# A rational-form attention on Trainium2: late key tiles ordered by a table of times, one exponential for two reciprocals, four banks in turn for the numerators

## The chip, the cores and the metric

The kernel runs on one core of one Trainium2 chip. The metric is the device time of one execution in microseconds (us); the profile's span is the time from the first to the last instruction of one profiled execution. Engine names are those of the profile: PE (matrix multiply), PEld (its weight loads), DVE (vector), ACT (activations), POOL (GpSimd), SP (the queue that issues most DMAs).

## The reference, cut to what matters

A network of two layers on x of shape (4, 128, 64, 64): a convolutional state-space layer, then an additive attention and a recurrent layer over 4096 tokens of 128 channels. The change touches the attention alone.

```python
def _L1_attn_ref(x, Wt, Wx, bh, Wa, ba):            # x: (4, 4096, 128), layer-normed tokens
    q = jnp.einsum('bld,ud->blu', x, Wt)            # 32 units u
    k = jnp.einsum('bld,ud->blu', x, Wx)
    beta = jnp.tanh(q[:, :, None, :] + k[:, None, :, :] + bh)
    alpha = jnp.einsum('bsju,u->bsj', beta, Wa[:, 0]) + ba[0]
    alpha = jnp.tanh(alpha)
    alpha = jax.nn.softmax(alpha, axis=-1)
    return jnp.einsum('bsj,bjd->bsd', alpha, x)

t = t + _L1_attn_ref(_ln_t(t), Wt, Wx, bh, Wa, ba)
t = t + _L1_ffn_ref(_ln_t(t), W, V, gamma, beta)
```

## The kernel before, in words

`_bounded` runs three stages one after the other, each with an order of instructions written out by hand: `_layer0` (the convolutional layer), `_rational` (the attention) and `_chunked` (the recurrent layer). The change is inside `_rational`.

The sum of tanh over 32 units is computed as a sum of fractions. The units are cut into groups of 6, 6, 5, 5, 5 and 5. For a group, exponentials of all signed sums of its units (64 or 32 rows) are kept for the keys (`F`) and for the queries (`E`). The product of `F` and `E` over the rows of a group is the fraction's denominator (`lower`, into a two-bank PSUM tile `pd`), and the product of `F` with the weighted `cE` is its numerator (`upper`, into two one-bank tiles `pn`). Unit A holds the two groups of 64 rows, B1 and B2 two groups of 32 rows each; B1 lies in rows 0 to 63 of PE's array, B2 in rows 64 to 127.

The work is tiled by batch `b` (4), by 512 queries (`s`, 8 per batch, so 32 query tiles) and by 128 keys (`jt`, 32 per query tile). For one `jt`:

- PE computes dA, dB1, dB2 (denominators) and nA, nB1, nB2 (numerators) (line 1212);
- ACT inverts each denominator by a logarithm (line 1231) and an exponential of its negative (line 1232), 1024 elements each, into `ra` (A) or `rb` (B1, B2);
- DVE multiplies with the numerators, two instructions of 512 elements per unit (`times`, line 1227; below xA, xB1, xB2);
- POOL adds B1 to A (line 1346; the first add), then B2 (line 1333; the second add);
- DVE adds the two halves into `A[:, jt, :]` (line 1343; below f).

The work of B2 and f belongs to the next pass of the loop over `jt`. So the order of one pass is: PE dA, nB2 of the pass before, dB1, nA, dB2, nB1; DVE xB2 of the pass before, xA, xB1, f of the pass before. The queues run in order; buffers set who waits. `psD` has two `pd` tiles, `psN` three `pn` banks, `psW` one bank (`ct`) for everything else; `ra` has three tiles, `rb` four.

At the end of a query tile ACT applies tanh and exp to `A` in four parts (lines 1381, 1382; another table is loaded before and the first one after, line 1068). Meanwhile `ahead` does the first `jt` of the next query tile with DVE reciprocals (`direct`, lines 1239, 1240), for which it needs the next `cE` (`weigh`, line 1200). The weighted sum over the keys (`weighted`, line 1357) is a chain of 32 matmuls into `ct`: the first 20 run at the end of the tile, the last 12 one by one in jt 2 to 13 of the next tile.

Other small pieces are hung into the loop by the dictionary `between`, behind the work of a given `jt`: the closing of the last query tile (copy of `ct`, a matmul for the softmax's denominators, four reciprocals, a matmul for the numerators, a POOL add and the output's DMA; `CLOSE_AT`), the layer norm of the next batch's tokens (`NORM_AT`: centre, square, rate, scale; not in the last batch) and the next tile's `E` (`QUERIES_AT`).

## Time and profile before

| What | Value |
|---|---|
| Time, median of 3 runs | 11655.28 us (11652.04 to 11657.58) |
| Profiled execution: its time | 11654.41 us |
| Profiled execution: span | 11652.7 us, mean granted PE clock 0.939 |
| Attention stage | about 4044 to 11430 us of the span, 32 query tiles |
| L1231, logarithm of 1024 (`rb`) | x1986, mean 1011 ns |
| L1232, exponential of 1024 (`rb`) | x1986, mean 1057 ns |
| L1382, exponential of 2048 (tile end) | x31, mean 1910 ns |
| L1227, DVE multiply of 512 (`rb`) | x3972, mean 682 ns |
| L1346 / L1333, POOL's first / second add of 1024 | x993 each, mean 2653 / 2363 ns |
| L1343, DVE's sum f | x993, mean 750 ns |
| L1239, DVE reciprocal of 512 | x186, mean 3351 ns |

The first stage (to about 4044 us) and the last one (from about 11430 us) hold none of the lines that the change touches. A line of the profile's timeline gives start, duration, engine, line, operation, output and input, count, and in brackets the idle time before it with what ended it; "L1212" is line 1212 of the kernel. Matmul durations overlap, so on PE the distance between starts is what counts.

### The profile page before, as it was taken

The page shows a single profiled execution, that of the slowest core. Times are in us where ns is not written, and L with a number is a line of the kernel's source. Part 1 is how long each engine was busy: PE and PEld are TensorE (multiplying, and loading weights), DVE is VectorE, ACT ScalarE, POOL GpSimd, SP SyncE. Part 2 cuts the span into 40 slices and gives each one's busy share as a digit, 9 for nine tenths or more (in the row PEclk, how much of TensorE's full clock was granted, in tenths as well). Part 3 has the DMA queues.
Part 4 walks back from the last instruction along what each step waited for, and adds up shares of the span by engine and source line. Part 5 has one row for each costly group of instructions (what it writes and reads, how often), then busy time and mean ns, then how long its engine had stood idle before and what let it go on. Part 6 is the DMA issues. An engine that isn't in the chain of part 4 may idle for free.

```text
span 11652.7 us, 111820 instructions
## 1 busy us (share of the span) xinstructions
PE 10307.6 (88%) x36210; PEld 3184.3 (27%) x36210; DVE 8997.6 (77%) x10066; ACT 9520.9 (82%) x10209; POOL 8625.1 (74%) x3703
## 2 busy tenths in 40 slices
PE   6787787778777699999999999999999999999997
PEld 2121121122111133333333333333333333333334
DVE  4998899889889677777777777777777777777773
ACT  3566556656655599999999999999999999999996
POOL 3999889889889677767766776767677767776773
PEclk8898898889888799999999999999999999999998
DMA  4888778778778300000000000000000000000001
GB/s 118 189 182 194 171 177 193 170 182 190 179 171 186 79 1 3 6 3 3 6 3 3 3 6 3 3 3 6 3 3 3 6 2 3 3 4 3 2 3 60
DMA packets 225332, 737.77 MB, mean 63 GB/s; under 512 B 41104, under 2 KB 41936, under 8 KB 223712
## 3 DMA queue, kind: packets, MB, share of 16 engines
q1 hardware_dynamic: 221760, 729.96, 26.5%
q8 instruction: 286, 4.69, 0.2%
q14 instruction: 310, 2.54, 0.1%
q10 hardware_dynamic: 2976, 0.58, 0.0%
HBM read 612.95 MB, written 117.44 MB: 63 GB/s over the span
## 4 chain that ended last, share of the span: by engine, by line
PE 50%; ACT 9%; DVE 4%; issue 3%; POOL 0%; DMA 0%; DVEq 0%; POOLq 0%; SPq 0%; ACTq 0%
PE pn L1212 26%; PE pd L1212 16%; PE ct L1357 4%; ACT A L1381 3%; ACT A L1382 2%; DVE rb L1227 2%; ACT rb L1231 1%; ACT rb L1232 1%; PE ct L1134 1%; ACT ra L1231 1%; DVE rb L1239 1%; PE vy L1556 0%; DVE A L1343 0%; PE pn L56 0%; PE ct L1262 0%
## 5 line engine op out<-in xcount | busy, mean ns | idle before, releaser
L1212 PE MATMUL pn<-cE,F 32*128 32x512 f32 (+1 forms) x12288 | 4728.8, 650 | 196.6 <-DVE rb L1227 88.5
L1227 DVE TENSOR_TENSOR rb<-rb,pn 128x512 f32<-128x512 f32 x3972 | 2544.5, 682 | 1310.9 <-PE pd L1212 684.9
L1212 PE MATMUL pd<-E,F 32*128 32x512 f32 (+1 forms) x12288 | 3478.0, 648 | 20.9 <-DVE ra L1239 15.7
L1346 POOL TENSOR_TENSOR ra<-ra,rb 128x1024 f32<-128x1024 f32 x993 | 2634.5, 2653 | 957.2 <-DVE rb L1227 956.9
L1333 POOL TENSOR_TENSOR ra<-ra,rb 128x1024 f32<-128x1024 f32 x993 | 2346.8, 2363 | 409.0 <-DVE rb L1227 348.4
L626 POOL TENSOR_TENSOR dBu<-dtdu,bbcc 128x1024 f32<-128x1024 f32 x1024 | 2398.3, 2368 | 216.9 <-DMA dtdu<-ddd 155.5
L1232 ACT ACTIVATE rb<-rb 128x1024 f32<-128x1024 f32 x1986 | 2099.6, 1057 | 62.8
L1212 PEld LDWEIGHTS pn<-cE,F 32*128 32x128 f32 (+1 forms) x12288 | 1418.0, 185 | 2574.8 <-DVE rb L1227 1066.6
L1231 ACT ACTIVATE rb<-pd 128x1024 f32<-128x1024 f32 x1986 | 2007.6, 1011 | 89.9 <-PE pn L1212 75.2
L668 PE MATMUL py<-h,gather 128*32 128x512 f32 x4096 | 1297.9, 699 | 477.3 <-POOL h L651 364.5
L1227 DVE TENSOR_TENSOR ra<-ra,pn 128x512 f32<-128x512 f32 x1986 | 1317.9, 684 | 231.4 <-ACT ra L1232 175.6
L1212 PEld LDWEIGHTS pd<-E,F 32*128 32x128 f32 (+1 forms) x12288 | 931.4, 185 | 1638.5 <-issue 693.7
L621 ACT ACTIVATE pa<-dtdu,a_neg 128x1024 f32<-128x1024 f32 x1024 | 1145.3, 1119 | 53.1 <-DVE h L641 32.1
L651 POOL TENSOR_TENSOR h<-h,bbcc 128x1024 f32<-128x1024 f32 x384 | 912.0, 2375 | 346.2 <-ACT carry L649 338.5
L641 DVE TENSOR_TENSOR_SCAN pa<-pa,carry,dBu 128x1024 f32<-128x1024 f32 x480 | 1124.7, 2343 | 23.1 <-ACT pa L621 11.3
L1232 ACT ACTIVATE ra<-ra 128x1024 f32<-128x1024 f32 x993 | 1049.6, 1057 | 31.4
L1357 PE MATMUL ct<-A,xT 128*128 128x512 f32 x2048 | 1050.9, 641 | 8.2 <-ACT A L1382 8.2
L1231 ACT ACTIVATE ra<-pd 128x1024 f32<-128x1024 f32 x993 | 1008.7, 1016 | 60.0 <-PE pd L1212 26.5
L649 ACT COPY carry<-pa 128x1 f32<-128x1 f32 x640 | 102.4, 160 | 1043.7 <-DVE h L648 1041.9
L1343 DVE TENSOR_TENSOR A<-ra 128x512 f32<-128x512 f32 x993 | 745.0, 750 | 116.3 <-POOL ra L1333 116.0
L648 DVE TENSOR_TENSOR h<-pa,bbcc 128x1024 f32<-128x1024 f32 x640 | 784.1, 1225 | 59.0 <-PE py L668 0.9
L641 DVE TENSOR_TENSOR_SCAN h<-pa,carry,dBu 128x1024 f32<-128x1024 f32 x288 | 675.0, 2344 | 171.1 <-PE py L668 148.2
(291 smaller groups left out, 8731.3 us busy)
## 6 DMA issues: line engine op xcount, KB each, us to landing
bbcc<-bcd SPq DMA_DIRECT2D x1024, 256.0 KB, 6.9
dtdu<-ddd SPq DMA_DIRECT2D x1024, 256.0 KB, 7.1
ddd<-dd SPq DMA_DIRECT2D x64, 1024.0 KB, 5.1
src<-src SPq DMA_DIRECT2D x64, 512.0 KB, 8.3
xs<-in_x_dram SPq DMA_DIRECT2D x16, 512.0 KB, 7.5
src<-xs SPq DMA_DIRECT2D x16, 512.0 KB, 3.0
bcd<-bc SPq DMA_DIRECT2D x64, 128.0 KB, 2.0
src<-xsT SPq DMA_DIRECT2D x16, 512.0 KB, 5.4
```

Of the source, the lines that this page charges most:

```text
L621: nc.scalar.activation(dA, its[m].DT[r][:, 0, :], AF.Exp, scale=a)
L626: nc.gpsimd.tensor_tensor(dBu, its[m].DT[r][:, 1, :], its[m].BC[q][:, 0, :], ALU.mult)
L641: nc.vector.tensor_tensor_scan(to[:, step], dA[:, step], live.pop(("dBu", u))[:, step], 0.0 if m % nch == 0 else its[m - 1].carry[:, col : ...
L651: nc.gpsimd.tensor_tensor(h, h, cc, ALU.mult)
L668: nc.tensor.matmul(it.y[to, c], gather, live["h", v][:, c], start=False, stop=(q == QS - 1))
L1212: nc.tensor.matmul(ps[a], F[lo:hi, i, jt * P : (jt + 1) * P], side[lo:hi, i, :], start=True, stop=True)
L1227: nc.vector.tensor_tensor(r[:, a, :], r[:, a, :], ns[a], ALU.mult)
L1231: nc.scalar.activation(r, d, AF.Ln, scale=LOWER)
L1232: nc.scalar.activation(r, r, AF.Exp, scale=-1.0)
L1333: nc.gpsimd.tensor_tensor(rA_, rA_, rB2_, ALU.add)
L1346: nc.gpsimd.tensor_tensor(rA, rA, rB1, ALU.add)
L1357: nc.tensor.matmul(ct, xT[:, jt, :], A[:, jt, :], start=(jt == 0), stop=(jt == JT - 1))
```

## The change

In short, as it stands in the diff:

- The loop over `jt` becomes a list of pieces with times. `steps` gives each piece of a key tile (d, n, ln, ex, x, the two adds a1 and a2, f) the time `jt` + an offset; the list is sorted and run in that order. `EARLY_STEPS` (jt below 14) keeps the old order of a pass; `LATE_STEPS` (jt 14 to 31) is another one.
- In the late table the order per `jt` is, on ACT: lnA, lnB1, exA, lnB2, exB, where exB is one exponential over B1 and B2 together (2048 elements); on PE: dA and dB1 one `jt` ahead, nB1 and nB2 one behind; on DVE: xB1, f (of two tiles before), xB2, xA.
- B1 and B2 share one `rb` tile of 2048 elements; the pool has three of them instead of four of 1024. The norm's square and the closing's reciprocal share one tile.
- The numerators' banks go in turn, three in the early part; when `ct` has been copied (time 13.95) its bank joins as the fourth. Queries, denominators and numerators of the closing take their bank from the same turn.
- The twelve weighted sums move from behind the work of jt 2 to 13 to a place between dB1 and nA (2.15 + i).
- The closing's reciprocal becomes a logarithm and an exponential on ACT at 15.4, and its end moves from 22 to 17.9; the norm's pieces move to 18.9, 20.4, 21.4 and 22.9.
- f of jt 30 and 31 (`sums`) goes behind the first reciprocals of the next query tile.

```diff
@@ -40,9 +40,21 @@
 QB = 512
 PARTS = ((0, 4), (4, 12), (12, 20), (20, 32))
 LAST_PARTS = ((0, 8), (8, 16), (16, 24), (24, 29), (29, 32))
-CLOSE_AT = (14, 16, 17, 18, 19, 20, 22)
-NORM_AT = (15, 17, 19, 20)
-QUERIES_AT = (24, 26)
+LATE = 14
+CLOSE_AT = (13.95, 15.4, 17.9)
+NORM_AT = (18.9, 20.4, 21.4, 22.9)
+QUERIES_AT = (24.9, 26.9)
+EARLY_STEPS = dict(
+    dA=0.00, dB1=0.10, nA=0.20, lnA=0.21, exA=0.22, xA=0.23, dB2=0.30, nB1=0.31, lnB1=0.40, exB1=0.41,
+    xB1=0.42, a1=0.44, lnB2=0.50, exB2=0.51, nB2=1.05, xB2=1.12, a2=1.13, f=1.43,
+)
+LATE_STEPS = dict(
+    dA=-0.44, dB1=-0.23, lnA=-0.12, lnB1=-0.04, exA=0.26, dB2=0.37, lnB2=0.50, nA=0.74, xA=0.81, exB=0.84,
+    nB1=1.11, xB1=1.38, nB2=1.42, xB2=1.49, a1=1.75, a2=1.88, f=2.46,
+)
 NOW = 20
 REACH = 21.0
 LOWER = 2.0**-13
@@ -1059,10 +1071,9 @@
     two = ctx.enter_context(tc.tile_pool(name="ntwo", bufs=2))
     sb = ctx.enter_context(tc.tile_pool(name="nsb", bufs=2))
     ra = ctx.enter_context(tc.tile_pool(name="nra", bufs=3))
-    rb = ctx.enter_context(tc.tile_pool(name="nrb", bufs=4))
+    rb = ctx.enter_context(tc.tile_pool(name="nrb", bufs=3))
     psD = ctx.enter_context(tc.tile_pool(name="npsD", bufs=2, space=PSUM))
-    psN = ctx.enter_context(tc.tile_pool(name="npsN", bufs=3, space=PSUM))
-    psW = ctx.enter_context(tc.tile_pool(name="npsW", bufs=1, space=PSUM))
+    psN = ctx.enter_context(tc.tile_pool(name="npsN", bufs=1, space=PSUM))
     def ln_exp():
         nc.scalar.preload_act_table_set("natural_log_exp_and_others")
@@ -1070,11 +1081,16 @@
     def pd():
         return psD.tile([P, 2, QB], F32, name="pd", tag="pd")
+    turns = {"taken": 0, "banks": 3}
     def pn():
-        return psN.tile([P, QB], F32, name="pn", tag="pn")
+        i = turns["taken"] % turns["banks"]
+        turns["taken"] += 1
+        return psN.tile([P, QB], F32, name=f"pn{i}", tag=f"pn{i}")
     def pw():
-        return psW.tile([P, QB], F32, name="ct", tag="ct")
+        return psN.tile([P, QB], F32, name="pn3", tag="pn3")
     w_t = k.load(wp, Wt, [U, P], "w_t")
@@ -1152,7 +1168,10 @@
             nc.vector.tensor_tensor(xc, xc, ps, ALU.subtract)
         def square():
-            held["sq"] = rb.tile([P, CH], F32, name="sq", tag="rb")[:, 0:n]
+            if n == QB:
+                held["sq"] = one.tile([P, QB], F32, name="sq", tag="rec")
+            else:
+                held["sq"] = four().rearrange("p a q -> p (a q)")[:, 0:n]
             nc.scalar.activation(held["sq"], xc, AF.Square)
         def rate():
@@ -1192,7 +1211,7 @@
         nc.vector.memset(xT[:, c * nt : (c + 1) * nt, 0:1], 1.0)
     def queries(E, xn, s, i):
-        exponent(pw(), w_q, xn[:, s * QB : (s + 1) * QB], i, E[:, i, :])
+        exponent(pn(), w_q, xn[:, s * QB : (s + 1) * QB], i, E[:, i, :])
     def weigh(E):
         cE = one.tile([P, 2, QB], F32, name="cE")
@@ -1226,21 +1245,67 @@
         for a in range(2):
             nc.vector.tensor_tensor(r[:, a, :], r[:, a, :], ns[a], ALU.mult)
-    def inverse(d, pool, tag):
-        r = pool.tile([P, 2, QB], F32, name=tag, tag=tag)
+    def log(r, d):
         nc.scalar.activation(r, d, AF.Ln, scale=LOWER)
+    def exp(r):
         nc.scalar.activation(r, r, AF.Exp, scale=-1.0)
-        return r
-    def direct(d, ns, pool, tag):
-        r = pool.tile([P, 2, QB], F32, name=tag, tag=tag)
+    def direct(r, d, ns):
         for a in range(2):
             nc.vector.reciprocal(r[:, a, :], d[:, a, :])
             nc.vector.scalar_tensor_tensor(r[:, a, :], r[:, a, :], 1.0 / LOWER, ns[a], ALU.mult, ALU.mult)
-        return r
-    def closing(b, s, ct, xr, parts):
+    def four():
+        return rb.tile([P, 4, QB], F32, name="rb", tag="rb")
+    def pair():
+        return ra.tile([P, 2, QB], F32, name="ra", tag="ra")
+    def steps(jt, F, E, cE, A, first):
+        h = {}
+        when = EARLY_STEPS if jt < LATE else LATE_STEPS
+        go = {}
+        def halves(u):
+            if "rb" not in h:
+                h["rb"] = four()
+            return h["rb"][:, 0:2, :] if u == "B1" else h["rb"][:, 2:4, :]
+        if first is None:
+            go["dA"] = lambda: h.update(dA=lower("A", F, jt, E))
+            go["dB1"] = lambda: h.update(dB1=lower("B1", F, jt, E))
+        else:
+            h["dA"], h["dB1"] = first
+        go["dB2"] = lambda: h.update(dB2=lower("B2", F, jt, E))
+        for u in ("A", "B1", "B2"):
+            go["n" + u] = lambda u=u: h.update({"n" + u: upper(u, F, jt, cE)})
+        def lnA():
+            h["ra"] = pair()
+            log(h["ra"], h["dA"])
+        go["lnA"] = lnA
+        go["exA"] = lambda: exp(h["ra"])
+        go["xA"] = lambda: times(h["ra"], h["nA"])
+        go["lnB1"] = lambda: log(halves("B1"), h["dB1"])
+        go["lnB2"] = lambda: log(halves("B2"), h["dB2"])
+        if jt >= LATE:
+            go["exB"] = lambda: exp(h["rb"])
+        else:
+            go["exB1"] = lambda: exp(halves("B1"))
+            go["exB2"] = lambda: exp(halves("B2"))
+        for u in ("B1", "B2"):
+            go["x" + u] = lambda u=u: times(halves(u), h["n" + u])
+        go["a1"] = lambda: nc.gpsimd.tensor_tensor(h["ra"], h["ra"], halves("B1"), ALU.add)
+        go["a2"] = lambda: nc.gpsimd.tensor_tensor(h["ra"], h["ra"], halves("B2"), ALU.add)
+        go["f"] = lambda: nc.vector.tensor_tensor(A[:, jt, :], h["ra"][:, 0, :], h["ra"][:, 1, :], ALU.add)
+        return [(jt + when[name] + (JT if name == "f" and jt >= JT - 2 else 0), f) for name, f in go.items()]
+    def closing(b, s, ct, xr, more):
         held = {}
@@ -1248,23 +1313,24 @@
             held["ct"] = one.tile([P, QB], F32, name="ct_s")
             nc.vector.tensor_copy(held["ct"], ct)
-        def denominators():
-            held["den"] = pw()
-            nc.tensor.matmul(held["den"], den_w, held["ct"], start=True, stop=True)
-            held["rec"] = one.tile([P, QB], F32, name="rec")
-        def invert(i):
-            cols = slice(i * QB // parts, (i + 1) * QB // parts)
-            nc.vector.reciprocal(held["rec"][:, cols], held["den"][:, cols])
+        def invert():
+            den = pn()
+            nc.tensor.matmul(den, den_w, held["ct"], start=True, stop=True)
+            held["rec"] = one.tile([P, QB], F32, name="rec", tag="rec")
+            if more:
+                nc.scalar.activation(held["rec"], den, AF.Ln)
+                exp(held["rec"])
+            else:
+                nc.vector.reciprocal(held["rec"], den)
         def end():
-            num = pw()
+            num = pn()
             nc.tensor.matmul(num, fix, held["ct"], start=True, stop=True)
             nc.vector.tensor_tensor(held["rec"], held["rec"], num, ALU.mult)
             nc.gpsimd.tensor_tensor(xr, xr, held["rec"], ALU.add)
             nc.sync.dma_start(x2[b, :, blocks[s]], xr)
-        return [take, denominators] + [lambda i=i: invert(i) for i in range(parts)] + [end]
+        return take, invert, end
     nn = L // CH
...
@@ -1309,45 +1375,27 @@
                 if s == 0:
                     upcoming = two.tile([P, L], F32, name="xn")
                 norm_load(b + 1, upcoming, blocks[s])
-                for at, go in zip(NORM_AT, norm_steps(upcoming, blocks[s], pn)):
-                    between.setdefault(at, []).append(go)
+                between += zip(NORM_AT, norm_steps(upcoming, blocks[s], pn))
             if more:
                 E_next = two.tile([P, 2, QB], F32, name="E")
                 of = upcoming if turned else xn
                 for i in range(2):
-                    between.setdefault(QUERIES_AT[i], []).append(
-                        lambda i=i, s=s, of=of, E_next=E_next: queries(E_next, of, (s + 1) % nq, i)
+                    between.append(
+                        (QUERIES_AT[i], lambda i=i, s=s, of=of, E_next=E_next: queries(E_next, of, (s + 1) % nq, i))
                     )
             ln_exp()
-            late = None
-            for jt in range(start, JT + 1):
-                if jt < JT:
-                    dA = lower("A", F, jt, E) if jt > start else first[0]
-                if late is not None:
-                    pj, rA_, rB2_ = late
-                    nB2 = upper("B2", F, pj, cE)
-                if jt < JT:
-                    dB1 = lower("B1", F, jt, E) if jt > start else first[1]
-                if late is not None:
-                    times(rB2_, nB2)
-                    nc.gpsimd.tensor_tensor(rA_, rA_, rB2_, ALU.add)
-                if jt < JT:
-                    nA = upper("A", F, jt, cE)
-                    rA = inverse(dA, ra, "ra")
-                    times(rA, nA)
-                    dB2 = lower("B2", F, jt, E)
-                    nB1 = upper("B1", F, jt, cE)
-                    rB1 = inverse(dB1, rb, "rb")
-                    times(rB1, nB1)
-                if late is not None:
-                    nc.vector.tensor_tensor(A[:, pj, :], rA_[:, 0, :], rA_[:, 1, :], ALU.add)
-                if jt == JT:
-                    break
-                nc.gpsimd.tensor_tensor(rA, rA, rB1, ALU.add)
-                rB2 = inverse(dB2, rb, "rb")
-                late = jt, rA, rB2
-                for go in between.pop(jt, ()):
-                    go()
+            between.append((CLOSE_AT[0], lambda: turns.update(banks=4)))
+            for jt in range(start, JT):
+                between += steps(jt, F, E, cE, A, first if jt == start else None)
+            between.sort(key=lambda e: e[0])
+            for _, go in between[:-2]:
+                go()
+            sums = [go for _, go in between[-2:]] if more else []
+            for _, go in between[-2:] if not more else ():
+                go()
+            turns["banks"] = 3
+            between = []
             if more:
                 E, cE = E_next, weigh(E_next)
@@ -1364,15 +1412,20 @@
                 if not more:
                     return
                 if step == 0:
-                    held["A"], held["B1"] = lower("A", F, 0, E), lower("B1", F, 0, E)
-                    held["A"] = direct(held["A"], upper("A", F, 0, cE), ra, "ra")
+                    dA, held["dB1"] = lower("A", F, 0, E), lower("B1", F, 0, E)
+                    held["A"], held["B"] = pair(), four()
+                    direct(held["A"], dA, upper("A", F, 0, cE))
+                    for go in sums:
+                        go()
                 elif step == 1:
-                    held["B2"] = lower("B2", F, 0, E)
-                    held["B1"] = direct(held["B1"], upper("B1", F, 0, cE), rb, "rb")
-                    nc.gpsimd.tensor_tensor(held["A"], held["A"], held["B1"], ALU.add)
+                    held["dB2"] = lower("B2", F, 0, E)
+                    r = held["B"][:, 0:2, :]
+                    direct(r, held["dB1"], upper("B1", F, 0, cE))
+                    nc.gpsimd.tensor_tensor(held["A"], held["A"], r, ALU.add)
                 elif step == 2:
                     held["first"] = lower("A", F, 1, E)
-                    r = direct(held["B2"], upper("B2", F, 0, cE), rb, "rb")
+                    r = held["B"][:, 2:4, :]
+                    direct(r, held["dB2"], upper("B2", F, 0, cE))
                     nc.gpsimd.tensor_tensor(held["A"], held["A"], r, ALU.add)
                 else:
                     held["first"] = held["first"], lower("B1", F, 1, E)
@@ -1396,14 +1449,12 @@
                 nc.vector.tensor_tensor(A[:, 0, :], held["A"][:, 0, :], held["A"][:, 1, :], ALU.add)
                 first = held["first"]
                 start = 1
-            between = {}
-            todo = closing(b, s, ct, xr, 4 if more else 1)
+            todo = closing(b, s, ct, xr, more)
             if more:
                 for i, jt in enumerate(range(NOW, JT)):
-                    between[2 + i] = [lambda jt=jt, weighted=weighted: weighted(jt)]
-                for at, go in zip(CLOSE_AT, todo):
-                    between[at] = [go]
+                    between.append((2.15 + i, lambda jt=jt, weighted=weighted: weighted(jt)))
+                between += zip(CLOSE_AT, todo)
             else:
                 for go in todo:
                     go()
...
```

The remaining edits only put the keys' and the transposes' pieces into the same list with times just before those of the old places.

## The prediction

> **What bounds the kernel now.** I read the page's head and slices, then the timeline of one attention tile, then busy times by stage, then single events.
>
> ```profile
> span 11652.7 us, 111820 instructions
> ...
> PE 10307.6 (88%) x36210; PEld 3184.3 (27%) x36210; DVE 8997.6 (77%) x10066; ACT 9520.9 (82%) x10209; POOL 8625.1 (74%) x3703
> ...
> ACT  3566556656655599999999999999999999999996
> ```
>
> From slice 15 on, ACT is full; the diff touches only this stage: 32 query tiles, from about 4044 to 11430 us. The table by stage, for the tile between two table loads of L1068 (4746.44 and 4975.27): jt 1-2; jt 3-13, each with a weighted-sum matmul (`ct`); jt 14-31; tile end.
>
> ```profile
> core 0: us, PE busy (x) PEld busy (x) DVE busy (x) ACT busy (x) POOL busy (x), PEclk, DMA share, GB/s
> 4746.44:4759.91 13.47, 12.88 (x51) 3.78 (x52) 7.72 (x13) 13.21 (x13) 7.67 (x4) 1.00 0.00 1
> 4759.91:4829.57 69.66, 69.66 (x290) 21.28 (x292) 49.05 (x77) 67.46 (x66) 55.24 (x23) 1.00 0.00 1
> 4829.57:4944.85 115.28, 112.28 (x446) 34.82 (x448) 88.40 (x135) 110.06 (x113) 92.61 (x39) 0.99 0.02 8
> 4944.85:4975.31 30.46, 26.58 (x68) 9.92 (x66) 26.50 (x17) 30.30 (x10) 6.83 (x3) 0.89 0.00 0
> ```
>
> jt 3-13 takes 69.66/11 = 6.33 us per jt; the timeline of ACT says how much of that ACT needs.
>
> ```profile
> 4764.05 1.02 ACT L1231 ACTIVATE rb<-pd 128x1024 f32<-128x1024 f32 x1
> 4766.24 1.02 ACT L1231 ACTIVATE ra<-pd 128x1024 f32<-128x1024 f32 x1
> ...
> 4914.24 0.58 ACT L1135 ACTIVATE E<-ct 128x512 f32<-128x512 f32 x1
> 4914.71 1.02 ACT L1231 ACTIVATE ra<-pd 128x1024 f32<-128x1024 f32 x1
> ...
> 4926.73 1.01 ACT L1231 ACTIVATE ra<-pd 128x1024 f32<-128x1024 f32 x1
> 4927.77 1.06 ACT L1232 ACTIVATE ra<-ra 128x1024 f32<-128x1024 f32 x1
> 4928.73 1.01 ACT L1231 ACTIVATE rb<-pd 128x1024 f32<-128x1024 f32 x1
> ...
> 4932.73 1.01 ACT L1231 ACTIVATE ra<-pd 128x1024 f32<-128x1024 f32 x1
> ```
>
> Free of waits (4926.73 to 4932.73) a jt costs ACT 6.00 us: three logarithms at 1.04 (each exponential waits for its own logarithm to end) and three exponentials at 0.96 (the next instruction starts 0.10 before they end). So jt 3-13 loses 0.33 each elsewhere: on PE.
>
> ```profile
> 4765.07 1.13 PE L1212 MATMUL pd<-E,F 64*128 64x512 f32 x4
> 4767.20 2.02 PE L1212 MATMUL pn<-cE,F 64*128 64x512 f32 x4
> 4768.10 0.29 PEld L1212 LDWEIGHTS pn<-cE,F 64*128 64x128 f32 x2 [0.61 <-DVE rb L1227]
> 4770.35 1.13 PE L1357 MATMUL ct<-A,xT 128*128 128x512 f32 x2
> ```
>
> PE is gapless there: 1.06 (dA) + 1.07 (nB2 beside dB1) + 1.95 (nA) + 1.19 (dB2 beside nB1) + 1.06 (ct) = 6.33. nA would take 1.06; its second half waits for the third `pn` bank, until DVE has used the first half of nB2. The late part's one long stall:
>
> ```profile
> 4879.90 2.36 POOL L1346 TENSOR_TENSOR ra<-ra,rb 128x1024 f32<-128x1024 f32 x1
> 4879.97 2.84 DVE L1343 TENSOR_TENSOR A<-ra 128x512 f32<-128x512 f32 x1 [0.41 <-POOL ra L1333]
> ...
> 4886.58 1.02 ACT L1231 ACTIVATE rb<-pd 128x1024 f32<-128x1024 f32 x1 [2.34 <-PE pn L1212]
> ...
> 4889.58 1.02 ACT L1231 ACTIVATE ra<-pd 128x1024 f32<-128x1024 f32 x1 [0.89 <-PE pd L1212]
> ```
>
> POOL, late by the norm's extra multiply (1.27), starts a first add as the second add ends; DVE's sum f then takes 2.84 instead of 0.69, and 3 us later ACT stands still for 2.34 + 0.89.
>
> **What the Trainium skill says.** "ScalarE: Activation LUTs", What ACT_TABLE_LOAD costs: an activation with immediates takes 186 ns + 0.833 ns per element, and back-to-back ones overlap by about 93 ns. The trace agrees (1057 ns at 1024, 1910 at 2048 elements, E's exponential 0.58 with 0.47 to its follower), except where the follower needs the result. "SBUF — State Buffer", Who interferes with whom: a DVE instruction with two SBUF inputs and a GpSimd instruction that reads SBUF exclude each other, and the first holds the ports to its end; the 2.84 agrees. "TensorE: Matmul & The Clock Gate", Part 3, The mechanism: matmuls keep their order and overlap where row groups differ: eight 32-row instructions took 1.07, as did four alone (4738.66 to 4739.72: 1.06). "TensorEngine Tiling (Array Packing)", Key Properties: a change of tiling mode drains the array: a ct pair costs 1.06 between other modes, 0.86 (2x0.43) inside a run.
>
> **Part 1: ct moved (jt 1-13).** At 2.15+i, ct now stands between dB1 and nA instead of after nB1; the rest of the early table keeps the old order. From dA's start: dA to 1.06, pair to 2.13, ct to 3.19. nB2's first half is used by DVE from 2.29 to 2.97, so both banks of nA are free at 3.19; nA ends 4.25. dB2 and nB1's first half start at 4.25; nB1's second bank is freed by xA's first half, 4.25+0.11+0.68 = 5.04, plus 0.06, and needs 0.86: 5.96. ACT needs 6.00, so I take 6.03. jt 1-13 now takes 83.13-1.30 (table load) = 81.83; 13x6.03 = 78.4: **-3.4**. Bounds: 0 if ct covers nothing, -3.8.
>
> **Part 2: late ACT (jt 14-31).** The order becomes lnA, lnB1, exA, lnB2, exB with one exponential of 2048. lnA and lnB1 are followed by independent work: 1.01-0.10 = 0.91 each; exA 0.96; lnB2 1.04; exB 1.91-0.09 = 1.82. Sum 5.64 per jt. Eighteen: 101.5. Kept extras: square 0.52, rate 1.24, two E at 0.48: 2.7. New on ACT: the denominator's logarithm and exponential, like the rate's, 1.24 (they replace four DVE reciprocals of 0.95, which delayed DVE only). Floor 105.5 against 115.28, if the others fit into 5.64:
> - PE loses one pairing (nB2 follows dB2, nB1 follows dB1 on the same rows): dB2 0.86, nB2 0.86, dA 1.06, nA 0.86, dB1 1.06, nB1 0.86 = 5.56. It fits by 0.08; if PE is late, nB1 and dB2 overlap again (-0.86).
> - DVE: six multiplies and f, 6x0.682+0.685 less 0.08 overlap each: 4.2. POOL: adds of 2.65 and 2.36 = 5.0, against 5.64 instead of 6.0-6.3. f must start between the end of the older tile's second add and POOL's next first add. From lnA's start: nB1 ends 6.69, xB1 8.04, first add 8.25-10.9, second add to 13.3, next xB1 ends 8.04+5.64 = 13.68. Margin 0.4.
> - Buffers: ra lives 2.6 jt of 3, rb 2.4 of 3; a pair of `pn` waits for the second pair before it, with four banks.
>
> Waits I add: the denominator's and the rate's matmul stand just before their logarithms (0.3 each), E's two matmuls end about 0.45 late: 1.5. Two POOL extras (output add at 17.9, norm scale at 22.9) each make POOL late by about 1.27 against a margin of 0.4: f is blocked by 2.2 twice. Bounds for one such event: 0.15 (worked forward through four banks and three buffers, where only lnB2 arrives late) and 3.4 (what the old one cost); I take 1.5, so 3.0. Changeover at jt 14: 0.6, bounds 0 and 2. Late part: 105.5+1.5+3.0+0.6 = 110.6: **-4.7**. Bounds: -9.2 (no events and no waits on matmuls) and +11 (the last rival).
>
> **Part 3: tile end.** The sums of jt 30 and 31 go behind the next tile's first reciprocals, so cE no longer waits for POOL (now 5.98 from the last exponential to the first reciprocal, 4944.84 to 4950.82). DVE gains about 1 us net. But ACT is gapless through 4944.85-4975.31 (busy 30.30 of 30.46) with the same tanh, exp and loads: **0**; bounds -0.3 and +0.5. PE's idle 3.72 before cE shortens on a queue nobody waits for.
>
> Other edits (square's buffer, larger rb tiles, table instead of loop) have no instruction of their own; no DMA is added; the output's store is issued about four jt earlier, past nothing on SP's queue.
>
> **Sum.** 8.1 per tile, about 8.0 with the eight tiles of the last batch, which have no norm event; 32x8.0 = 256. The profiled execution took 11654.4 for a span of 11652.7, the median of the runs is 11655.3: 11655-256 = **11399**.
>
> **Rivals.**
> - *Nothing stalls*: 3.4+9.2 = 12.6 per tile, 403: 11252. For: four banks, spare DVE time. Against: POOL's margin of 0.4.
> - *Late jt stays at 6.0*, PE or POOL setting it, since PE's 5.56 has 0.08 to spare and blocked sums may alternate: 108.0+2.7+1.2+1.5 = 113.4, -1.9; with the early part 5.3 per tile, 170: 11485. If instead the early part gains nothing: 4.7x32 = 150: 11505.
> - *Slower: the blocked sum sustains itself.* Once POOL starts its first add the moment its second ends, f loses every time: first add 2.36, f 0.74, xB2 1.2 and 0.2 of signalling, second add 2.36: 6.9 per jt. From jt 17 to 31: 15x(6.9-5.64) = 18.9 in place of the 3.0: late 126.5, +11.2, less 3.4: +7.8 per tile, 250: 11905. It decides when jt 17-31 average over 5.64 + (115.28+3.4-107.6)/15 = 6.38. For: the margin of 0.4 and two extras on POOL. Against: xA and xB1 (2.5) after xB2 end about as the second add does, which lets f in again; before, it recovered after one loss.
> - *The change does nothing* (waits hold the old order): against it, each wait on ACT in the new order is for its own operands.
>
> **How the numbers follow.** My forecast (gain 200-330) 0.50; nothing stalls 0.15; late or early gain missing (50-200) 0.22; slower 0.10; no change 0.03. Predicted 11399. The range takes in both neighbours with their ends, 11250 to 11530, and leaves out the slower case and part of the best. A difference under 0.2% (23 us) can't be told from no change: faster 0.87, same 0.03, slower 0.10.
>
> **What would show it.** Right: starts of the `ra` logarithm 6.0 apart in jt 3-13, no pn wait over 0.2 there; 5.64 apart late, outside extras; the 2048-element exponential near 1.9; tile end still 30.4; tiles of about 221 us. Wrong: `f` near 2.8 in most late jt, ACT waiting for DVE (ra) or for PE (pd) in the late part, 6.3 left early.

## The result, and the profile after

The changed kernel takes 11658.65 us (median of 12 runs, 11642.16 to 11683.33), the kernel before in the same session 11652.92 (11648.98 to 11657.78): ratio 1.0004, 95% interval 0.9995 to 1.0013. I had predicted 11399. The profiled execution took 11652.02 us. The page's head:

```profile
span 11650.3 us, 108806 instructions
...
PE 10226.8 (88%) x36210; PEld 3317.8 (28%) x36210; DVE 9190.3 (79%) x9942; ACT 9353.7 (80%) x9695; POOL 8595.5 (74%) x3703
```

ACT is busy for 167 us less than before (9520.9), in a span that is 2.4 us shorter: what it was spared came back as waiting. The table by stage shows where, first for a tile of the commonest length (jt 1-2, jt 3-13, late part, tile end), then the late part of another tile (stretch and its length; busy time and count of PE, PEld, DVE, ACT, POOL; PE's granted clock; DMA):

```profile
4728.35:4743.13 14.78, 14.78 (x58) 4.61 (x60) 9.77 (x14) 13.56 (x13) 7.37 (x4) 1.00 0.00 0
4743.13:4811.43 68.30, 68.30 (x289) 19.92 (x292) 49.01 (x78) 66.20 (x68) 55.23 (x23) 1.00 0.00 1
4811.43:4923.23 111.80, 108.71 (x443) 39.66 (x443) 87.70 (x129) 105.59 (x99) 89.98 (x38) 0.97 0.02 8
4923.23:4953.64 30.41, 23.69 (x66) 8.77 (x65) 29.88 (x19) 30.26 (x9) 9.28 (x4) 0.94 0.00 0
...
5490.09:5609.20 119.11, 114.80 (x443) 41.00 (x443) 89.58 (x129) 106.06 (x98) 89.55 (x38) 0.90 0.02 7
```

ACT's busy time in the late part is what I had worked out (105.5), but the part lasts 111.80 in one tile and 119.11 in another with the same instructions. Beside PE's busy time, the column that differs is PE's granted clock, 0.97 and 0.90. Summed over the 32 late parts, the record of the clock shows 0.5 (below: half clock) for 134 us before and 433 us after. Means of tiles 1 to 31 (counted from 0), before and after: from table load to jt 14, 83.15 and 83.36; late part 114.71 and 114.69. The tile end takes 30.42 in both, except where a batch ends.

Before has half clock too: behind the blocked sum that the prediction shows, the closing's matmul took 1.82, not 1.13 (the record shows 0.5 from 4884.7 to 4888.1).

```profile
4886.66 1.82 PE L1262 MATMUL ct<-ct_s,fix 128*128 128x512 f32 x2
```

**What starts it, place one.** The timeline of POOL, DVE, PE and ACT around jt 20 and 21 of the first of these tiles:

```profile
4848.47 2.37 POOL L1303 TENSOR_TENSOR ra<-ra,rb 128x1024 f32<-128x1024 f32 x1
4850.78 2.37 POOL L1302 TENSOR_TENSOR ra<-ra,rb 128x1024 f32<-128x1024 f32 x1
...
4850.87 2.82 DVE L1304 TENSOR_TENSOR A<-ra 128x512 f32<-128x512 f32 x1 [0.61 <-POOL ra L1303]
4853.62 1.27 DVE L1246 TENSOR_TENSOR rb<-rb,pn 128x512 f32<-128x512 f32 x2
...
4854.35 1.29 PE L1231 MATMUL pn<-cE,F 32*128 32x512 f32 x3 [1.15 <-DVE rb L1246]
...
4856.21 2.08 PE L68 MATMUL pn<-sq,avg 128*128 128x512 f32 x2
4858.22 2.08 PE L1231 MATMUL pn<-cE,F 32*128 32x512 f32 x4
4860.23 2.08 PE L1231 MATMUL pd<-E,F 64*128 64x512 f32 x4
...
4858.32 0.69 ACT L83 ACTIVATE sq<-pn,eps 128x512 f32<-128x512 f32 x1 [1.65 <-PE pn L68]
```

Read downwards: POOL starts the next first add (L1302) as the second (L1303) ends, so f (L1304) loses the ports and takes 2.82 instead of 0.69 (below: a blocked sum). Behind it xB2 is late, and with it the `pn` bank that PE needs next: PE stands still for 1.15. Less than 2 us later its matmuls take 2.08 instead of 1.13 or 1.02, and ACT waits for PE: 1.65 here, 1.03 a jt later.

The blocked sum costs time without the half clock too. In tile 8 the same f takes 2.83 and PE stands still for as long, but its matmuls keep full speed:

```profile
6009.35 2.83 DVE L1304 TENSOR_TENSOR A<-ra 128x512 f32<-128x512 f32 x1 [0.60 <-POOL ra L1303]
...
6012.83 1.29 PE L1231 MATMUL pn<-cE,F 32*128 32x512 f32 x3 [1.15 <-DVE rb L1246]
...
6014.49 1.13 PE L68 MATMUL pn<-sq,avg 128*128 128x512 f32 x2
...
6015.66 0.69 ACT L83 ACTIVATE sq<-pn,eps 128x512 f32<-128x512 f32 x1 [0.50 <-PE pn L68]
```

Three late parts of the changed kernel have no half clock at all, those of tiles 8, 16 and 24. They still take 3.1, 3.1 and 4.3 longer than the same tiles of d_half, the best version below.

**Place two**, jt 15, PE and ACT in the tile that lasts 119.11:

```profile
5496.89 1.55 PE L1231 MATMUL pd<-E,F 32*128 32x512 f32 x4 [0.77 <-ACT ra L1249]
5498.36 2.08 PE L1318 MATMUL pn<-ct_s,den_w 128*128 128x512 f32 x2
...
5500.48 0.60 ACT L1321 ACTIVATE rec<-pn 128x512 f32<-128x512 f32 x1 [1.78 <-PE pn L1318]
...
5508.05 1.02 ACT L1249 ACTIVATE rb<-pd 128x1024 f32<-128x1024 f32 x1 [2.52 <-PE pd L1231]
```

Nothing is blocked here. PE is ahead and waits 0.77 for ACT to free a `pd`; then the closing's matmul takes 2.08. In the tile of 111.80 the idle time at the same place is 0.16, and the same matmul takes 1.13:

```profile
4818.22 1.13 PE L1231 MATMUL pd<-E,F 32*128 32x512 f32 x4 [0.16 <-ACT ra L1249]
4819.27 1.13 PE L1318 MATMUL pn<-ct_s,den_w 128*128 128x512 f32 x2
```

Twelve of the 32 tiles have this stretch. Seven others have the same idle time and keep full speed, as tile 2 does:

```profile
4592.92 1.13 PE L1231 MATMUL pd<-E,F 32*128 32x512 f32 x4 [0.78 <-ACT ra L1249]
4593.98 1.13 PE L1318 MATMUL pn<-ct_s,den_w 128*128 128x512 f32 x2
```

What differs is the moment. In the record of the clock of one run, the half-clock stretches of the attention begin on one grid of 3.41 us and last multiples of it. Measured from the grid line before it, the idle time of jt 15 began at 1.10 to 2.37 us in the twelve tiles, and at 0.53 to 0.60 or 2.55 to 2.86 in the seven. Five of the runs (after and, below, sums_first, no_f_late, no_pool_extras and half_adds) have this idle time, in 95 tiles together: half clock followed in all 60 in which it began 1.05 to 2.43 us after a grid line, and in none of the other 35.

The Trainium skill, "TensorE: Matmul & The Clock Gate", section A second HAM failure mode: psum-queue depth-cycling, says that short idle times between groups of matmuls can make the clock swing between half and full; the trace agrees. The table in the page's section Why this matters for your kernels warns of idle times of more than about 3 us; here one of 0.77 was enough where it fell at the wrong moment, and the measurement decides. PE's late chain needs 5.56 of 5.64 per jt at full clock, so at half clock ACT waits at once.

**Place three**, the tile end (POOL, DVE, then ACT):

```profile
4925.35 2.36 POOL L1302 TENSOR_TENSOR ra<-ra,rb 128x1024 f32<-128x1024 f32 x1
4927.79 2.43 POOL L1303 TENSOR_TENSOR ra<-ra,rb 128x1024 f32<-128x1024 f32 x1
...
4925.64 4.87 DVE L1219 TENSOR_SCALAR cE<-E,c_n 128x512 f32<-128x512 f32 x2
4930.43 3.35 DVE L1257 RECIPROCAL ra<-pd 128x512 f32<-128x512 f32 x1
...
4957.89 1.02 ACT L1249 ACTIVATE rb<-pd 128x1024 f32<-128x1024 f32 x1 [0.84 <-PE pd L1231]
```

cE no longer waits for POOL's sums; it runs beside them, and its two instructions take 4.87 instead of 0.88. The first reciprocal starts 7.2 after the last exponential (4923.21), before the change 5.98, and jt 1 takes 7.51 in the mean instead of 6.02.

### The profile page after: what moved, and what is told of

Its sections match the earlier page's. It is cut to its first block, busy times and chain, and to the rows that moved or that the text cites. A ratio compares the mean times of both kernels' runs of the same rounds, so it can differ in the third digit from the quotient of the medians.

```text
span 11650.3 us, 108806 instructions
## 1 busy us (share of the span) xinstructions
PE 10226.8 (88%) x36210; PEld 3317.8 (28%) x36210; DVE 9190.3 (79%) x9942; ACT 9353.7 (80%) x9695; POOL 8595.5 (74%) x3703
## 4 chain that ended last, share of the span: by engine, by line
PE 44%; DVE 8%; ACT 7%; POOL 4%; issue 3%; DMA 0%; POOLq 0%; DVEq 0%; SPq 0%; ACTq 0%
PE pn L1231 18%; PE pd L1231 15%; PE pn L1405 7%; ACT rb L1249 3%; POOL ra L1303 2%; POOL ra L1302 2%; DVE rb L1246 2%; DVE ra L1257 2%; ACT ra L1249 2%; ACT ra L1252 1%; DVE cE L1219 1%; DVE A L1304 1%; PE pn L1150 1%; PE pn L68 1%; DVE rb L1257 1%
## 5 line engine op out<-in xcount | busy, mean ns | idle before, releaser
L1231 PE MATMUL pn<-cE,F 32*128 32x512 f32 (+1 forms) x12288 | 3875.3, 641 | 100.0 <-DVE rb L1246 54.8
L1302 POOL TENSOR_TENSOR ra<-ra,rb 128x1024 f32<-128x1024 f32 x993 | 2607.4, 2626 | 992.1 <-DVE rb L1246 964.5
L1246 DVE TENSOR_TENSOR rb<-rb,pn 128x512 f32<-128x512 f32 x3972 | 2575.1, 681 | 706.4 <-PE pd L1231 376.1
L1303 POOL TENSOR_TENSOR ra<-ra,rb 128x1024 f32<-128x1024 f32 x993 | 2348.2, 2365 | 398.1 <-DVE rb L1246 315.3
L1252 ACT ACTIVATE rb<-rb 128x1024 f32<-128x1024 f32 (+1 forms) x1410 | 1982.4, 1406 | 44.8
L1231 PEld LDWEIGHTS pn<-cE,F 32*128 32x128 f32 (+1 forms) x12288 | 1297.3, 190 | 1989.5 <-DVE rb L1246 841.4
L1246 DVE TENSOR_TENSOR ra<-ra,pn 128x512 f32<-128x512 f32 x1986 | 1271.9, 681 | 533.1 <-PE pn L1231 515.0
L1304 DVE TENSOR_TENSOR A<-ra 128x512 f32<-128x512 f32 x993 | 965.5, 975 | 168.0 <-POOL ra L1303 161.7
L1405 PE MATMUL pn<-A,xT 128*128 128x512 f32 x2048 | 1048.7, 640 | 6.9 <-ACT A L1435 6.9
```

The lines of the kernel that those rows point to most:

```text
L1231: nc.tensor.matmul(ps[a], F[lo:hi, i, jt * P : (jt + 1) * P], side[lo:hi, i, :], start=True, stop=True)
L1246: nc.vector.tensor_tensor(r[:, a, :], r[:, a, :], ns[a], ALU.mult)
L1252: nc.scalar.activation(r, r, AF.Exp, scale=-1.0)
L1302: go["a1"] = lambda: nc.gpsimd.tensor_tensor(h["ra"], h["ra"], halves("B1"), ALU.add)
L1303: go["a2"] = lambda: nc.gpsimd.tensor_tensor(h["ra"], h["ra"], halves("B2"), ALU.add)
L1304: go["f"] = lambda: nc.vector.tensor_tensor(A[:, jt, :], h["ra"][:, 0, :], h["ra"][:, 1, :], ALU.add)
```

## The experiments

Times are medians; "ratio" is against the kernel before, run in the same session (for after 11652.9, for the others 11656.6 to 11657.9), with its 95% interval. Early (table load to jt 14), late and jt 1 are means over tiles 1 to 31 of the profiled execution; "half" is half-clock time in all 32 late parts, from the first logarithm of jt 14 to the table load behind jt 31. The expectations below count it over slightly different stretches: 428 for after, 253 for den_first.

| Kernel | us | ratio | early | late | jt 1 | half |
|---|---|---|---|---|---|---|
| before | 11653 | | 83.15 | 114.71 | 6.02 | 134 |
| after | 11659 | 1.0004 (0.9995 to 1.0013) | 83.36 | 114.69 | 7.51 | 433 |
| sums_first | 11665 | 1.0004 (0.9998 to 1.0011) | 83.57 | 115.22 | 7.74 | 451 |
| den_first | 11577 | 0.9931 (0.9915 to 0.9948) | 83.41 | 112.15 | 7.57 | 262 |
| no_f_late | 11475 | 0.9844 (0.9828 to 0.9861) | 83.29 | 109.94 | 7.48 | 167 |
| no_pool_extras | 11620 | 0.9968 (0.9959 to 0.9977) | 83.85 | 112.67 | 8.01 | 228 |
| early_all | 11811 | 1.0132 (1.0115 to 1.0149) | 81.36 | 121.62 | 6.12 | 520 |
| d_half | 11346 | 0.9734 (0.9718 to 0.9751) | 81.46 | 106.77 | 6.10 | 3 |
| d_guard | 11373 | 0.9760 (0.9743 to 0.9776) | 82.40 | 106.74 | 6.55 | 7 |
| d_early_cE | 11685 | 1.0026 (1.0016 to 1.0036) | 83.61 | 115.31 | 6.89 | 365 |
| half_adds | 11410 | 0.9793 (0.9776 to 0.9809) | 81.39 | 108.30 | 6.07 | 85 |
| before_half | 11627 | 0.9972 (0.9963 to 0.9982) | 83.43 | 113.58 | 6.05 | 57 |
| d_half_guard | 11384 | 0.9767 (0.9751 to 0.9783) | 82.32 | 107.00 | 6.53 | 3 |
| d_half_ct_back | 11406 | 0.9787 (0.9771 to 0.9803) | 83.36 | 106.85 | 6.07 | 3 |

**den_first**: is it the idle time of PE?

```diff
-CLOSE_AT = (13.95, 15.4, 17.9)
+CLOSE_AT = (13.95, 15.36, 17.9)
```

> The denominator's matmul is issued before dB2 of jt 15 instead of after it, where PE stands idle for 0.2 to 0.8 us. Theory B (an idle gap of PE of 0.5 us or more sets PE to half clock for 3.4 us and more, and that is what makes late parts long): the slow matmuls at jt 15 and 16, which 12 of the 32 tiles have, are gone, about 4 us in each of these: 11610, and half-clock time in late parts under 350 us instead of 428. Rival (the half clock comes from the late order's matmuls themselves, gap or none): it stays at jt 15 and 16 in as many tiles; only ACT's wait of 0.4 for the denominator goes, 13 us: 11645.

The matmul now stands in the gap before dB2. In the tile that had lasted 119.11, PE and ACT show:

```profile
5491.62 1.12 PE L1318 MATMUL pn<-ct_s,den_w 128*128 128x512 f32 x2 [0.28 <-DVE ra L1246]
5492.68 1.13 PE L1231 MATMUL pd<-E,F 32*128 32x512 f32 x4
...
5493.81 0.60 ACT L1321 ACTIVATE rec<-pn 128x512 f32<-128x512 f32 x1
```

No wait on ACT, full clock, and the stretch at jt 15 is gone from all twelve tiles; this one's late part takes 111.54. One matmul moved by one place in the order gives 82 us (11659 to 11577), more than the 50 expected. The stretch had a sequel: in after, exactly these twelve tiles also have a blocked sum at jt 17, and in den_first none has. The rival is out: the same matmuls run at full clock once the gap is filled.

**no_f_late and no_pool_extras**: is it the blocked f, and what blocks it?

```diff
-        go["f"] = lambda: nc.vector.tensor_tensor(A[:, jt, :], h["ra"][:, 0, :], h["ra"][:, 1, :], ALU.add)
+        m = QB if jt < LATE else 8
+        go["f"] = lambda: nc.vector.tensor_tensor(A[:, jt, 0:m], h["ra"][:, 0, 0:m], h["ra"][:, 1, 0:m], ALU.add)
```

> The sum f of jt 14 to 31 is cut to 8 of its 512 columns, so these columns alone are summed; A's others hold zeros at first. Theory C (a blocked f delays nB1's bank, which gives PE its gap at jt 21 and then the half clock): no f takes over 0.4, no PE gap over 0.5 at jt 21, half-clock time in late parts under 150 us, late parts of 107 to 109: about 6.5 x 32 = 210 us less: 11450. Rival (PE's chain of unpaired products or the pn banks limit the late part, f or none): late parts stay at 112 and more; 11560 or more.

```diff
-            nc.gpsimd.tensor_tensor(xc, xc, held["sq"], ALU.mult)
+            if n > QB:
+                nc.gpsimd.tensor_tensor(xc, xc, held["sq"], ALU.mult)
...
-            nc.gpsimd.tensor_tensor(xr, xr, held["rec"], ALU.add)
+            if not more:
+                nc.gpsimd.tensor_tensor(xr, xr, held["rec"], ALU.add)
```

> The norm's multiplication by the rate (GpSimd, 512 columns) and the addition of the residual at the output are left out, except in the prologue and the last tile. Theory C' (the two extras make GpSimd late, and so f loses the ports in the jt after them): under 40 blocked sums instead of 134, no gap at jt 21, late parts about 4 us shorter: 11530. Rival (f loses the race by chance in any jt): as many blocked sums, at other jt, 11640 to 11660.

Without most of f the late parts of 15 of the tiles 1 to 23 take 107.8 to 108.6 and no half clock is left at jt 21; it stays at jt 15 in 16 tiles. Half of the expectation failed: even the f of 8 columns took 2.3 at jt 20 and 21, so the ports are lost there too. It costs nothing, presumably because DVE has 0.5 less to do in each jt; this run doesn't part the two. And without POOL's two extra instructions as many sums are blocked (154 over 1.5 us, after: 140), most of them in jt 20 to 24 as before. So the extras don't cause it, and 11620 lies in neither of the forecast's ranges. Two adds of 2.36 and f's 0.69 take 5.41 of every 5.64, which leaves little room. Why the losses begin where they do stays open: DVE's own extra work near there, the closing's multiply at 17.9, stood in every run. Eleven tiles of no_pool_extras show again what blocked sums cost by themselves: with no half clock and four or five blocked sums in each late part, they take 2.1 to 3.4 longer than the same tiles of d_half.

**d_half and d_guard**: two ways to keep a lost race from costing anything, both on top of den_first.

```diff
+        def add(u):
+            for a in range(2):
+                nc.gpsimd.tensor_tensor(h["ra"][:, a, :], h["ra"][:, a, :], halves(u)[:, a, :], ALU.add)
```

> With the denominator's matmul moved as in den_first (11577): in the late part each of GpSimd's additions of 1024 columns is two of 512. Theory C (a blocked f waits for the addition that holds the ports, and so delays nB1's bank by its length): a blocked f takes 1.7 to 1.9 instead of 2.8, PE's gap at jt 21 falls under 0.5, half-clock time in late parts from 253 to under 120 us, late parts of 109 to 110: 11500 to 11530. Rival (GpSimd's own time sets jt 20 to 24: four additions of 1.28 are 0.4 longer than two of 2.36): late parts 113 to 116, 11600 to 11680.

```diff
+        if jt > LATE:
+            one_ = lambda: halves("B1")[:, 0, 0:1]
+            go["g"] = lambda: nc.vector.tensor_scalar(one_(), one_(), 1.0, None, ALU.mult)
...
-    nB1=1.11, xB1=1.38, nB2=1.42, xB2=1.49, a1=1.75, a2=1.88, f=2.46,
+    nB1=1.11, xB1=1.38, nB2=1.42, xB2=1.49, a1=1.75, a2=1.88, g=1.47, f=2.46,
```

> With the denominator's matmul moved as in den_first (11577): in the late part a multiplication of one element by 1.0 stands behind each f on VectorE, in the buffer that GpSimd's next first addition reads, so that this addition can't start before f has ended. Theory C: no f in jt 15 to 31 is blocked by a first addition (none of 2.8), no gap over 0.5 at jt 21; but f's 0.7 is now in GpSimd's loop: 2.36 + 2.36 + 0.75 + 0.1 + 0.2 = 5.75 in jt that are late: 11490 to 11550. Rival (f merely makes visible that GpSimd is late, and the loop of additions with f inside is what limits jt 20 to 24): late parts 112 or more, 11577 or more.

Both beat the forecast: 311 and 284 us faster than the kernel before. In part that is the early part, which the forecast left out: in d_half it is 1.95 per tile shorter than in den_first, about 60 us. d_half at jt 20 and 21 (DVE, PE, ACT), and the late part of the tile that after had taken 111.80 for, in the table by stage:

```profile
4847.03 1.74 DVE L1310 TENSOR_TENSOR A<-ra 128x512 f32<-128x512 f32 x1
...
4846.72 1.13 PE L68 MATMUL pn<-sq,avg 128*128 128x512 f32 x2
4847.78 1.13 PE L1231 MATMUL pn<-cE,F 32*128 32x512 f32 x4
...
4847.89 0.69 ACT L83 ACTIVATE sq<-pn,eps 128x512 f32<-128x512 f32 x1 [0.42 <-PE pn L68]
```

```profile
4803.10:4910.52 107.42, 106.49 (x440) 38.81 (x440) 90.89 (x129) 105.26 (x98) 96.99 (x71) 1.00 0.02 8
```

f is still blocked, and more often (its mean is 1089 ns, after: 975), but for 1.75 at most, not 2.82: the add that holds the ports is half as long. PE has no gap there, its clock is 1.00, and ACT's idle time in the late part falls from 6.2 to 2.2, though POOL is busy for 7 us more. In d_guard f is hardly ever blocked (two of 1024 over 1.5 us, mean 706 ns): the same late part by another way. Its jt 1 is helped less (6.55 against 6.10; cE still takes 3.0), and so d_half is the faster by 27.

**half_adds and before_half**: which part of this is the change's? half_adds is d_half's edit with `CLOSE_AT` as the change has it. before_half is the kernel before with:

```diff
-                    nc.gpsimd.tensor_tensor(rA_, rA_, rB2_, ALU.add)
+                    for a in range(2) if pj >= 14 else (slice(0, 2),):
+                        nc.gpsimd.tensor_tensor(rA_[:, a, :], rA_[:, a, :], rB2_[:, a, :], ALU.add)
...
-                nc.gpsimd.tensor_tensor(rA, rA, rB1, ALU.add)
+                for a in range(2) if jt >= 14 else (slice(0, 2),):
+                    nc.gpsimd.tensor_tensor(rA[:, a, :], rA[:, a, :], rB1[:, a, :], ALU.add)
```

> The changed kernel with GpSimd's additions halved in the late part, and the denominator's matmul where the change has it. Theory C with B: the blocked sums' gap at jt 20 to 24 is gone as in d_half, the gap before dB2 of jt 15 stays, and sets PE to half clock in about a third of the tiles at about 4 us each: 11 to 13 tiles, 50 us over d_half's 11346: 11395. Rival (only both together free the late part): 11500 or more.

> The kernel before, with GpSimd's additions of jt 14 to 31 halved and nothing else. Theory (the one blocked sum per tile was all that could be had there: 2.34 + 0.89 of ScalarE's waiting in the 24 tiles with a norm; its jt is set by ScalarE's 6.00): 3 x 24 = 72 to 100 us: 11555 to 11585. So the change itself, with the blocked sums mended in both, would be worth 160 us or more. Rival (the halved additions alone bring what d_half brought, the late order nothing): under 11450.

The halved adds alone bring the changed kernel to 11410, and the kernel before only to 11627, short of the 11555 to 11585 that I had expected. With this one fault mended in both, the change is worth 217 us. It was there, and the blocked sums with the half clock behind them hid it. Nine tiles of half_adds keep the stretch at jt 15, which is den_first's 64 us.

**early_all**: is the late order worth its trouble as it stands?

```diff
-LATE = 14
+LATE = 32
```

> The early table for all 32 jt: the late order with its shared exponential is undone, the rest of the change kept (closing on ScalarE, deferred sums, the weighted products' new place). Theory D (the late order has gained little in all, since its half clock and blocked sums have eaten what ScalarE was spared): late parts of 18 x 6.0 to 6.2 and 4 us of extras, 112 to 116, and the time within 60 us of the changed kernel's 11658. Rival (the late order as such costs time): 100 us or more faster than the changed kernel, under 11560. Rival (the late order gains 4 a tile after all, and something else has taken it): 100 us slower, over 11760.

The second rival holds: without the late order the kernel is 152 us slower, late parts of 121.6 with the most half clock of all (520 us). But it is also 154 slower than the kernel before, whose order per jt it shares. So the rest of the change, with closing and norm placed for the late table, costs time under the early one, and 152 is no measure of the late order alone. The 217 us between half_adds and before_half measure the change as a whole.

**sums_first and d_early_cE**: the tile end.

```diff
-            sums = [go for _, go in between[-2:]] if more else []
-            for _, go in between[-2:] if not more else ():
-                go()
+            sums = []
+            for _, go in between[-2:]:
+                go()
```

> The last two additions and sums of a tile run before cE again, everything else as in the changed kernel. Theory A (cE is held by GpSimd's last additions, and what DVE loses there comes out as the wait in jt 1): the two cE take about 0.9 instead of 4.9, jt 1 takes 6.0 to 6.3 instead of 7.3, so about 1.1 x 31 = 35 us less than the changed kernel's 11658: about 11623. Rival (DVE's chain is late whichever way the sums stand): jt 1 stays over 7, 11650 to 11660.

```diff
+                cE_next = two.tile([P, 2, QB], F32, name="cE")
+                for i in range(2):
+                    between.append((28.47 + i, lambda i=i, E_=E_next, c_=cE_next: weigh(E_, c_, (i,))))
...
-                E, cE = E_next, weigh(E_next)
+                E, cE = E_next, cE_next
```

> With the denominator's matmul moved as in den_first (11577): cE is computed in jt 28 and 29 behind f, into a second buffer; the deferred sums stay. (The residual's load comes at jt 19 instead of the tile's start, into one buffer instead of two, and the set-up's weights share buffers, to make room.) Theory E (VectorE's chain from the last exponential to A0's sum is what makes jt 1 late: four multiplies of the shared exponential, cE and six reciprocals): the first reciprocal starts 2.5 after the last exponential instead of 7.2, jt 1 takes 6.0 to 6.3 instead of 7.3, 1.1 x 31 = 35 us: 11540. Rival (jt 1 is late by PE's order at the tile end): jt 1 stays at 7.0 or more, 11570 to 11580.

Both theories fall as I had put them. In sums_first cE does take 0.88, but the first reciprocal starts 8.7 after the last exponential (4933.68 to 4942.37), later than in either kernel: the shared exponential of jt 31 puts four multiplies behind it (2.48, before two in 1.28), and POOL's adds come after these. In d_early_cE the first reciprocal starts 2.7 after it, as expected, but jt 1 takes 6.89 in the mean, and cE beside POOL at jt 28 takes 2.59 and costs the late part 3.2; the run is 108 us slower than den_first, on which it stands. PE of d_early_cE, at the start of a tile, tells why jt 1 is not mended:

```profile
4979.89 0.70 PE L1235 MATMUL pd<-E,F 32*128 32x512 f32 x2 [1.82 <-ACT ra L1253]
...
4981.70 2.07 PE L1235 MATMUL pn<-cE,F 32*128 32x512 f32 x2 [0.68 <-DVE ra L1250]
4983.70 2.08 PE L1235 MATMUL pd<-E,F 64*128 64x512 f32 x4
```

PE was done early, waited 1.82 for ACT's first logarithm behind the table load, and met the tile at half clock, as in 20 of the 31 tiles. It is not the whole cause: seven tiles without this wait have jt 1 at 6.57 to 7.99. d_half has jt 1 at 6.10: the first reciprocal comes 4.75 after the last exponential, cE takes 1.89, and the chain of reciprocals ends just before the table load.

**d_half_ct_back and d_half_guard**: the weighted products' place, and both mendings together.

```diff
-                    between.append((2.15 + i, lambda jt=jt, weighted=weighted: weighted(jt)))
+                    between.append((2.35 + i, lambda jt=jt, weighted=weighted: weighted(jt)))
```

> d_half with the weighted products of jt 20 to 31 after dB2 and nB1 again (the place that they had in the kernel before) instead of between dB1 and nA. Theory (their new place shortens PE's chain from 6.33 to 6.21): jt 2 to 13 take 6.33, so 0.12 x 12 x 31 = 45 us more: 11391. Rival (what my prediction said, 6.03 against 6.33): 0.3 x 12 x 31 = 110 us: 11457. Rival (the place does nothing): 11346.

> d_half and d_guard together. Theory (in d_half the blocked sums that are left, of 1.4 to 1.8, are hidden): the guard removes them and changes the late part's 106.8 by less than 0.5: 11335 to 11360. Rival (they still cost): late parts of 105.5, 11300 to 11315. Rival (four additions, f and the guard's wait in one loop are over 5.64): 11400 or more.

With the products in their old place a jt takes 6.33 again, against 6.21: 60 us, nearer to 45 than to 110. It is more than 45 because in most tiles of d_half jt 2 to 5 take 6.0 to 6.1. Both mendings together are no better than one: the late part stays (107.00), the early part is longer (82.32 against 81.46, with jt 1 at 6.53), and 11384 lies in none of the ranges that I had given. The best version is d_half, 311 us under the kernel before; its four runs lie within 3.1 us, those of after within 41.

## Why the prediction was wrong, by its own steps

- **What bounds the kernel** (ACT from slice 15 on): right, and half of it. PE's 5.56 against 5.64 was read as "it fits by 0.08", at full clock. The prediction has no term for a slower clock, though before's own timeline had matmuls at half clock behind its blocked sum.
- **Part 1, ct moved, -3.4**: right in sign, mis-sized: 6.21 instead of 6.03. The term is nB1's second half: xA starts 0.17 after nA's end, not 0.11, and the half takes 1.05, not 0.86. What is left is worth 12 x 0.12 = 1.4 per tile, and jt 1, not looked at, took it back (7.51 - 6.02 = 1.5).
- **Part 2, late ACT, -4.7**: the floor was exact (ACT busy 105.59 for 105.5; 5.63 per jt free of waits, for 5.64), and so were the 1.5 of waits: floor and waits make 107.0, and d_half, without long blocked sums and half clock, takes 106.8. The step that failed is what happens when POOL and PE are late or early. It was put at two POOL events of 1.5, caused by POOL's extras. The runs show 4.4 blocked sums per tile, most in jt 20 to 24, which come without the extras too. Without any half clock the late part still loses about 3 (tiles 8, 16 and 24: 3.1, 3.1 and 4.3), some 0.5 of it to the place of the closing's matmul (by which the tiles of half_adds without half clock lie over those of d_half), the rest to blocked sums. So the 3.0 was near by luck. What had no term is PE's half clock. The late parts of after exceed those of d_half by 7.9 in the mean; less the 3 this leaves about 5 per tile for it, an estimate from these figures. The changeover at 0.6 failed in twelve tiles, where PE's 0.77 of idle time at jt 15 set off the half clock: den_first's 82 us are 2.6 per tile.
- **Part 3, tile end, 0**: the tile end itself was right (30.42 in both). "DVE gains about 1 us net" failed: it loses 1.2, by cE's 4.87 beside POOL. The Trainium skill, "SBUF — State Buffer", Who interferes with whom, which I had cited for f, has this too: it lists `tensor_scalar`, which cE is, among the operations that can enter a two-port mode and then contend with GpSimd. The 4.87 agrees. I applied the section to f and not to cE.
- **The sum of 8.1 per tile**: half_adds shows 83.15 - 81.39 + 114.71 - 108.30 = 8.2, and 11410 us, near the predicted 11399. That nearness is luck: the early part gave 1.8 instead of 3.4 and the late part 6.4 instead of 4.7, with an edit that the prediction did not have. Of the mechanism, ACT's part was right; the blocked sums and PE's half clock cancelled it.
- **The rivals**: none named the clock. The slower one, f that blocks itself, had the right place. The chain did not run on to jt 31, but in 18 of the 32 tiles f is blocked at jt 20 and again at jt 21; blocked sums cost time by themselves, and they set off the half clock. In d_half more sums are blocked, for 1.75 at most, and next to nothing is lost.

## What to carry to other kernels

When one engine is made faster until a second has no room, ask what the second does in its new idle moments: here a PE that stood still for about 1 us often ran at half clock for the next 3.4 us and more, and part of the gain went back. Fill such a gap with work that is due anyway, or close it. Where VectorE and GpSimd share ports, a lost race cost f about the length of the add that held them (2.82 beside adds of 2.36, 1.74 beside halved ones), so cut that instruction before reordering.

## What the runs showed of the hardware that I had not expected

- Idle times of PE of 0.5 to 1.65 us, in a loop otherwise full, were often followed by matmuls at half speed (2.08 for 1.13, 1.92 for 1.02) within 3 us. For the 0.77 of jt 15 the moment on a grid of 3.41 us decided whether it happened, 60 of 60 against 0 of 35.
- The profile's record of the clock and the durations of the matmuls agree: at jt 21 of the first tile above, the matmuls are slow from 4856.2 to about 4862, and the record shows 0.5 from 4855.8 to 4862.6. A table by stage over narrow windows finds such a stretch.
- POOL's work in four instructions of 512 costs 7 us more of its time per tile than in two of 1024, and was still worth 249 us.
